# A new order of the words that drive all engines in a fused cross-attention kernel, with other places for its loads

## The chip, the cores and the metric

The kernel runs on one core of a Trainium2 chip. The metric is the device time of one execution in microseconds (us), as the median of several runs. Engines are named as in the profile: PE is TensorE (PEld its weight loads), DVE is VectorE, ACT ScalarE, POOL GpSimd, and SP is SyncE, which here issues nearly all DMAs.

## The reference

Everything is fp32: x is 2 x 2048 x 640, the context 2 x 154 x 1024, of which 77 rows are text and 77 image prompt. There are 20 heads of 32. Two softmaxes over 77 keys each are summed:

```python
q = _split_heads(hidden_states @ Wq.T, H)
k = _split_heads(text @ Wk.T, H)
v = _split_heads(text @ Wv.T, H)
out_text = _merge_heads(_attend(q, k, v, sm_scale))
k_ip = _split_heads(ip @ Wk_ip.T, H)
v_ip = _split_heads(ip @ Wv_ip.T, H)
out_ip = _merge_heads(_attend(q, k_ip, v_ip, sm_scale))
out = out_text + IP_SCALE * out_ip
out = out @ Wo.T + bo
return out + residual
```

## The kernel before

**Tiling.** Channels stand on the partitions. The work is cut into 10 pairs q (batch x chunk of 128 channels, that is four heads), each pair into two units u = 2q, 2q + 1 (half of the 2048 tokens), and each unit's eight 128-token tiles into three groups s (three, three and two tiles). Scores of a group lie in four PSUM banks, one per head (`halves`, or single `banks`); the softmax rows lie in SBUF in `pb`, 128 x 1848 for a group of three. The values of a pair are spread into the buffer `v4_0` or `v4_1` (by the pair's parity), as blocks for the attention run. The output product (Wo) uses sums of blocks of both factors, so that fewer products are needed; this part ends the program.

**The order.** Nothing here is scheduled by the framework. After a head that is written out (L523 to L558: the first loads, 40 small matmuls and projections), the string `SCHEDULE` (L561 to L625) holds one word for each step, and `emit` (L631) issues the instructions of a word in the order of the string. Each engine takes its own instructions in that order, so the string sets the order on PE, DVE, ACT, POOL and SP's DMA queue at once; semaphores add the waits for data and for buffers that come free. The words that are spoken of below:

- `Rs.u@h`: scores of group s of unit u (`scores`, L225), 24 matmuls, or 16 for group 2 (L232)
- `q.u.h`: query projection for 512 tokens, 5 chunks, which are 10 matmuls in the trace (`queries`, L197; L200), and `cq` its copy on ACT
- `k.c.t`, `v.c.t`: key and value projection of a chunk (`project_kv`, L137; L141), with `ck`, `cv` the copies
- `A.q`: the attention run of a pair (`attend`, L324; L331), 160 matmuls of 32 x 32 weights; `CA.q` its copy
- `K` copy of scores from PSUM to SBUF (L244, ACT), `M` maximum (L280, DVE), `S` subtraction of it (L294, POOL), `E` exponential (L300, or one by one with a bias, L268, ACT), `D` sum (L305, DVE), `I` reciprocal (L310), `N` normalisation (L315, POOL), `T` transposition (L322, DVE)
- `m`, `o`, `p`, `z`, `F`: products and sums of the output stage; `G`, `W` sums of blocks for it; `SF`, `SS` fetch and store of parts of the output, 256 KB each
- loads on SP: `LQ.q` a chunk of Wq into one of three buffers `wq_0` to `wq_2` (L191, 320 KB), `LK.n` a projection weight into one of four parts of `aT` (L131, 512 KB), `LX.u.h` a block of x of the second batch into one of `x_0` to `x_2` (L185, 1280 KB), `LO` all of Wo (L163, 1600 KB), `VS.q.half` eight small DMAs that spread v into the buffer `v4` of the pair (L157, 20 KB each; they wait until the run of pair q - 2 has read it)

A load waits on SP for its buffer, and everything behind it on SP waits with it. `DIRECT`, `BIASED` and `SUMMED` choose for a group how its softmax is taken: DIRECT reads scores from PSUM without the copy, BIASED leaves out the subtraction and gives the maximum as a bias to the exponential, SUMMED lets the exponential add up the rows.

Of the kernel before, what the change touches and what calls it, by code (L numbers as in the profile page):

```python
# [9 lines left out]
F32 = mybir.dt.float32  # L10
# [10 lines left out]
def kernel(  # L21
# [43 lines left out]
        (11, 0), (12, 0), (13, 0), (13, 2), (14, 0), (14, 2), (15, 1), (15, 2), (16, 2), (18, 1), (19, 2),  # L65
    }
    BIASED = {
        (3, 2), (4, 2), (5, 2), (6, 0), (8, 2), (9, 2), (10, 2), (12, 2), (18, 2),
    }
    SUMMED = {  # L70
        (4, 2), (10, 2), (12, 0), (12, 2), (13, 0), (13, 2), (14, 0), (15, 1), (15, 2), (16, 2), (18, 1),
        (18, 2),
# [480 lines left out]
    for t in range(2):  # L553
# [216 lines left out]
    for c, stages in enumerate(chains_of):  # L770
        for _, text in stages:
            for _, t in terms(text):
                for h in range(NH):
                    o = int(t[0]), NH * int(t[1]) + h
# [115 lines left out]
```

## Time and profile before

| what | value |
|---|---|
| median of 3 runs | 500.02 us (499.75 to 500.19) |
| profiled execution | 503.24 us |
| its span | 501.4 us |
| granted TensorE clock, mean | 0.997 |
| PE busy | 492.5 us |
| instructions in the trace | 10438 |

The span is the time from the first to the last record of the trace, and 1.8 us of the profiled execution lie around it. Rows of instruction groups read: line, engine, operation, output <- input, count, busy time and mean of one, then the idle time before it and what ended it. The chain rows read: start, length, engine, output, line, count. The rows on SP show DMA issues: start, length, engine, line, output <- input, count. q8 is the queue that brings TensorE its instructions, in packets.

### The profile page before, as it was taken

The numbers are of one execution on the slowest core, as the hardware profiler recorded it, in microseconds if no ns is written. First come the engines' busy times: TensorE is split into PE (matmuls) and PEld (weight loads), VectorE is DVE, ScalarE is ACT, GpSimd is POOL, SyncE is SP. The second block draws the span as 40 slices with busy tenths as digits, with TensorE's granted clock in tenths as the row PEclk, the third lists the DMA queues.
The fourth block names the chain that finished last, engine by engine and source line by source line (L and its number), as shares of the span: only waits on it lengthen the run. The fifth ranks groups of instructions, "written<-read, shape, count | busy, mean of one in ns | idle before, by whom it ended". The sixth has DMA issues, their size and how long they took to land.

```text
span 501.4 us, 10438 instructions
## 1 busy us (share of the span) xinstructions
PE 492.5 (98%) x4114; PEld 289.9 (58%) x4114; DVE 410.4 (82%) x411; ACT 303.2 (60%) x967; POOL 377.0 (75%) x167
## 2 busy tenths in 40 slices
PE   8999999999999989999999999999999999999996
PEld 4666658567457547446646654666655685444442
DVE  0069989979999987978997887678799999989785
ACT  1166768977797776757989887586677961100000
POOL 0069999878979886969976678556899899686950
PEclk9999999999999998999999999999999999999999
DMA  8991351060253560476552666653661122310125
GB/s 253 354 291 37 107 158 43 22 186 2 54 154 121 169 216 5 144 259 230 179 190 77 187 195 250 176 177 94 218 184 42 44 86 86 127 63 22 42 84 209
DMA packets 67473, 69.38 MB, mean 138 GB/s; under 512 B 5472, under 2 KB 47200, under 8 KB 67424
## 3 DMA queue, kind: packets, MB, share of 16 engines
q1 hardware_dynamic: 66704, 68.00, 43.1%
q8 instruction: 32, 0.52, 0.5%
q10 hardware_dynamic: 720, 0.72, 0.4%
q14 instruction: 17, 0.14, 0.1%
HBM read 54.94 MB, written 10.49 MB: 130 GB/s over the span
## 4 chain that ended last, share of the span: by engine, by line
PE 94%; DMA 3%; SPq 1%; issue 1%; ACT 0%; DVE 0%
PE bank L200 32%; PE bank L847 11%; PE bank L331 11%; PE bank L232 11%; PE bank L489 10%; PE bank L141 9%; PE bank L470 7%; PE bank L499 3%; DMA aT<-in_L_xattn_Wk_ip_dram 2%; DMA wq<-in_L_xattn_Wq_dram 2%; SPq L533 1%; SPq L131 0%; DVE x L793 0%; ACT pb L244 0%; ACT kT L558 0%
## 5 line engine op out<-in xcount | busy, mean ns | idle before, releaser
L315 POOL TENSOR_TENSOR pb<-pb,rden 128x1848 f32<-128x1848 f32 (+1 forms) x60 | 176.2, 2942 | 34.2 <-DVE rden L310 32.7
L200 PE MATMUL bank<-x,wq 128*128 128x512 f32 x400 | 179.5, 598 | 1.2 <-DMA wq<-in_L_xattn_Wq_dram 0.6
L294 POOL TENSOR_TENSOR pb<-pb,mx 128x1848 f32<-128x1848 f32 (+1 forms) x40 | 124.0, 3108 | 57.3 <-DVE mx L280 57.0
L200 PEld LDWEIGHTS bank<-x,wq 128*128 128x128 f32 x400 | 73.8, 190 | 87.1 <-issue 78.0
L322 DVE STREAM_TRANSPOSE pb<-pb 128x1920 f32<-128x1920 f32 (+1 forms) x60 | 116.1, 1940 | 6.0 <-POOL pb L315 5.5
L280 DVE TENSOR_REDUCE mx<-pb 128x24 f32<-128x1848 f32 (+1 forms) x49 | 90.4, 1854 | 34.8 <-ACT pb L244 34.6
L244 ACT COPY pb<-bank 128x462 f32<-128x462 f32 (+1 forms) x196 | 83.9, 543 | 32.4 <-PE bank L232 31.9
L305 DVE TENSOR_REDUCE den<-pb 128x24 f32<-128x1848 f32 (+1 forms) x48 | 90.1, 1883 | 14.0 <-ACT pb L300 13.8
L300 ACT ACTIVATE pb<-pb 128x1848 f32<-128x1848 f32 (+1 forms) x40 | 67.0, 1675 | 24.6 <-POOL pb L294 24.5
L268 ACT ACTIVATE pb<-bank,mx 128x77 f32<-128x77 f32 x224 | 64.0, 384 | 12.0 <-DVE mx L283 12.0
L232 PEld LDWEIGHTS bank<-kT,qT 32*128 32x128 f32 x1280 | 46.0, 185 | 29.7 <-issue 18.7
L232 PE MATMUL bank<-kT,qT 32*128 32x154 f32 x1280 | 57.5, 307 | 2.5 <-issue 2.2
L331 PE MATMUL bank<-pb,v 32*32 32x512 f32 x1600 | 55.5, 597 | 0.0
L141 PE MATMUL bank<-wo_ct,aT 128*128 128x154 f32 x320 | 47.1, 304 | 0.3 <-DMA aT<-in_L_xattn_Wk_ip_dram 0.3
L141 PEld LDWEIGHTS bank<-wo_ct,aT 128*128 128x128 f32 x320 | 44.4, 194 | 3.1 <-issue 2.1
L268 ACT ACTIVATE pb<-pb,mx 128x77 f32<-128x77 f32 x152 | 44.7, 389 | 1.1 <-DVE mx L280 1.1
L268 ACT ACTIVATION_READ_ACCUMULATOR pb<-bank,mx 128x1 f32 x168 | 43.6, 265 | 0.0
L331 PEld LDWEIGHTS bank<-pb,v 32*32 32x32 f32 x1600 | 30.0, 103 | 22.9 <-issue 12.9
L470 PE MATMUL bank<-aT,wo_ct 128*128 128x512 f32 x80 | 36.4, 596 | 0.0
L210 ACT ACTIVATE qT<-bank 128x512 f32<-128x512 f32 x40 | 23.9, 612 | 19.8 <-PE bank L200 19.7
L489 PE MATMUL bank<-aT,wo_ct 128*128 128x256 f32 x128 | 32.3, 387 | 0.0
L489 PEld LDWEIGHTS bank<-aT,wo_ct 128*128 128x128 f32 x128 | 23.6, 190 | 7.7 <-issue 4.0
(74 smaller groups left out, 439.1 us busy)
## 6 DMA issues: line engine op xcount, KB each, us to landing
x<-in_x_dram SPq DMA_DIRECT2D x20, 1280.0 KB, 7.5
out_dram<-acc SPq DMA_DIRECT2D x20, 256.0 KB, 3.0
x<-in_x_dram SPq DMA_DIRECT2D x18, 256.0 KB, 5.8
acc<-in_x_dram SPq DMA_DIRECT2D x16, 256.0 KB, 4.9
out_dram<-x SPq DMA_DIRECT2D x15, 256.0 KB, 2.1
v<-vS SPq DMA_DIRECT2D x160, 20.0 KB, 2.6
wq<-in_L_xattn_Wq_dram SPq DMA_DIRECT2D x9, 320.0 KB, 4.0
aT<-in_L_xattn_Wk_dram SPq DMA_DIRECT2D x5, 512.0 KB, 5.9
```

What stands on the lines that cost most here:

```text
L141: nc.tensor.matmul(keys_in(out), loaded[n][:, k, :], cT[:, k, :, t, :], start=(k == 0), stop=(k == NCC - 1))
L200: nc.tensor.matmul(pq, wqs[q % 3][:, k, :], xs[place_of(u, h)][:, k, :], start=(k == 0), stop=(k == NC - 1),)
L232: nc.tensor.matmul(ps[g][:, ts(t, 2 * L)], qTs[(u, h)][g * D : (g + 1) * D, ts(st, P)], kT[g * D : (g + 1) * D, c, b].rearrange("p t l -> ...
L244: nc.scalar.copy(keys_of(u, s)[:, :, g], ps[g][:, : n * 2 * L].rearrange("p (n l) -> p n l", n=n))
L268: nc.scalar.activation(row, row if ps is None else rows_in(ps[g], n)[:, t, x], AF.Exp, bias=maxs[(u, s)][:, *one], accum_out=None if den i ...
L280: nc.vector.tensor_reduce(mx, rows_of(u, s), AX.X, ALU.max, negate=negate)
L294: nc.gpsimd.tensor_tensor(rows_of(u, s), rows_of(u, s), maxs[(u, s)].unsqueeze(3).to_broadcast([P, n, 2, L]), ALU.subtract)
L305: nc.vector.tensor_reduce(den_of(u, s), rows_of(u, s), AX.X, ALU.add)
L315: nc.gpsimd.tensor_tensor(rows_of(u, s), rows_of(u, s), rdens[(u, s)].unsqueeze(3).to_broadcast([P, n, 2, L]), ALU.mult)
L322: nc.vector.transpose(p, p)
L331: nc.tensor.matmul(pa[r][g * D : (g + 1) * D, :], v4s[q % 2][rows, g, k, :], zones[rows, :, g, k, :], start=(k == 0), stop=(k == NK - 1),)
L489: nc.tensor.matmul(part, w_of[m][:, kp, op], t_of(m, b, i)[:, kp], start=(op == kp == 0 and m in (1, 2, 5)), stop=(op == 1 and kp == 1 and ...
```

## The change

`SCHEDULE` is replaced by another order of nearly the same words (1030 instead of 1025); everything that moves is in this string and in the three sets. TensorE has the same 4114 matmuls. There are 51 words K instead of 49, 42 S instead of 40, 49 D instead of 48. The head stays as it is. The new set `SUMMED` has one row less, so every line of the kernel after it has a number that is one less.

```diff
     DIRECT = {
-        (11, 0), (12, 0), (13, 0), (13, 2), (14, 0), (14, 2), (15, 1), (15, 2), (16, 2), (18, 1), (19, 2),
+        (11, 0), (12, 0), (13, 0), (13, 2), (15, 1), (15, 2), (16, 2), (18, 1), (19, 2),
     }
     BIASED = {
-        (3, 2), (4, 2), (5, 2), (6, 0), (8, 2), (9, 2), (10, 2), (12, 2), (18, 2),
+        (3, 2), (4, 2), (6, 2), (8, 2), (9, 2), (11, 2), (12, 1), (14, 0), (18, 2),
     }
     SUMMED = {
-        (4, 2), (10, 2), (12, 0), (12, 2), (13, 0), (13, 2), (14, 0), (15, 1), (15, 2), (16, 2), (18, 1),
-        (18, 2),
+        (4, 2), (11, 2), (12, 0), (13, 0), (13, 2), (14, 0), (15, 1), (15, 2), (18, 1), (18, 2), (19, 2),
     }
```

One line of the string, at the third attention run, from before and of the change:

```diff
-        "N1.7 M0.8 R1.8@1 q.10.0@2 K1.8 LX.11.0 T1.7 S0.8 M1.8 E0.8 A.3@1 LX.10.1 D2.8 S1.8 cq.9.1 D0.8 cq.10.0 "
+        "M0.8 R1.8@1 G5.0 q.10.0@3 LX.11.0 T1.7 K1.8 S0.8 cq.9.1 M1.8 E0.8 A.3@1 D2.8 S1.8 cq.10.0 D0.8 I0.8 E1.8 "
```

**SP around the run A.1.** Before, in the order of SP's DMAs: the spreads of pair 1, then `LQ.4`, `LK.14`, `LK.12`, `LQ.5`, `LK.11`, and spreads of pair 2. `LQ.5` and `LK.11` stand behind the word A.1 in the string, the three before them ahead of it.

```order
L157 DMA v4_1_81<-vS0_1_94 32x160 x16
L191 DMA wq_1_76<-in_L0_xattn_Wq_dram 128x5x128
L131 DMA aT_86<-in_L0_xattn_Wv_dram 128x8x128
L131 DMA aT_86<-in_L0_xattn_Wk_dram 128x8x128
L191 DMA wq_2_77<-in_L0_xattn_Wq_dram 128x5x128
L131 DMA aT_86<-in_L0_xattn_Wv_ip_dram 128x8x128
L157 DMA v4_0_80<-vS0_0_93 32x160 x8
```

After, at the same place (the first row is the second half of pair 1's spreads): `LK.14`, `LK.12` and `LQ.5` stand ahead of A.1, and the next load, `LK.15`, behind the run and the scores that follow it.

```order
L156 DMA v4_1_81<-vS0_1_94 32x160 x8
L130 DMA aT_86<-in_L0_xattn_Wv_dram 128x8x128
L130 DMA aT_86<-in_L0_xattn_Wk_dram 128x8x128
L190 DMA wq_2_77<-in_L0_xattn_Wq_dram 128x5x128
L130 DMA aT_86<-in_L0_xattn_Wv_ip_dram 128x8x128
L156 DMA v4_0_80<-vS0_0_93 32x160 x8
```

`LQ.4` has moved behind A.1, some rows further down, and `LQ.5` ahead of the run. On TensorE the projection right ahead of A.1 is `q.6.0` (buffer `wq_0`) where it was `q.5.1` (buffer `wq_2`); `q.5.1` now stands ahead of the scores `R1.4`.

**SP from the run A.3 to the run A.4.** Before: half of pair 3's spreads, then `LX.11.0` and `LX.10.1` (x_2, x_0), the first ahead of A.3, the second right behind it; the spreads of pair 4 around `LX.12.0`; then, ahead of A.4, a fetch, `LX.12.1` and `LO`, and the spreads of pair 5.

```order
L157 DMA v4_1_81<-vS0_1_94 32x160 x8
L185 DMA x_2_84<-in_x_dram 128x5x512
L185 DMA x_0_82<-in_x_dram 128x5x512
L157 DMA v4_0_80<-vS0_0_93 32x160 x8
L185 DMA x_1_83<-in_x_dram 128x5x512
L157 DMA v4_0_80<-vS0_0_93 32x160 x8
L458 DMA res_88<-in_x_dram 128x512
L185 DMA x_2_84<-in_x_dram 128x5x512
L163 DMA wo_ct_96<-in_L0_xattn_Wo_dram 128x5x640
L157 DMA v4_1_81<-vS1_95 32x160 x16
```

After: the spreads of pair 3, `LX.11.0`, half of pair 5's spreads, `LX.10.1`, `LQ.6`, `LX.12.0`, the sixteen spreads of pair 4, and then, ahead of A.4, `LX.12.1`, `LO`, `LX.13.0` and `LX.14.0`; the last row, `LX.13.1`, stands behind the run.

```order
L156 DMA v4_1_81<-vS0_1_94 32x160 x16
L184 DMA x_2_84<-in_x_dram 128x5x512
L156 DMA v4_1_81<-vS1_95 32x160 x8
L184 DMA x_0_82<-in_x_dram 128x5x512
L190 DMA wq_0_75<-in_L0_xattn_Wq_dram 128x5x128
L184 DMA x_1_83<-in_x_dram 128x5x512
L156 DMA v4_0_80<-vS0_0_93 32x160 x16
L184 DMA x_2_84<-in_x_dram 128x5x512
L162 DMA wo_ct_96<-in_L0_xattn_Wo_dram 128x5x640
L184 DMA x_0_82<-in_x_dram 128x5x512
L184 DMA x_1_83<-in_x_dram 128x5x512
L184 DMA x_2_84<-in_x_dram 128x5x512
```

`LX.10.1` has moved past the spreads of pair 5, which wait for the run A.3, since that run reads the buffer `v4_1`. `LX.13.0` and `LX.14.0`, which stood behind the word A.4 and the spreads of pair 5, now stand ahead of that run. Around A.7, `LX.18.1` stands behind the run's word in both orders, and in the new one right behind the eight spreads of `VS.8.0`, which stood some words further up.

124 rows, old and new, of the table SCHEDULE are left out of this document.

## The prediction

> **What bounds the kernel now.** I read the page's busy times first, then the shares of the chain that ended last, then what TensorE (PE) waited for.
>
> ```profile
> PE 492.5 (98%) x4114; PEld 289.9 (58%) x4114; DVE 410.4 (82%) x411; ACT 303.2 (60%) x967; POOL 377.0 (75%) x167
> ...
> PE 94%; DMA 3%; SPq 1%; issue 1%; ACT 0%; DVE 0%
> ...
> PE bank L232 <- issue: 2.2, 2, 1.7
> ```
>
> TensorE is busy for 98% of the span and the chain is TensorE for 94%. The 4114 matmuls are the same before and after, so only three things can move the time: pauses of TensorE, its clock, and what it pays at the joints between kinds of work. The third row is the largest pause behind the head: two waits in the scores, 2.2 us together, for nothing that the profile shows ("issue"). The timeline of TensorE gives their places, the windows what lies between them (columns: length; busy us and instructions of PE, PEld, DVE, ACT, POOL; granted clock; DMA share; GB/s):
>
> ```profile
> 113.80 0.53 PE L232 MATMUL bank<-kT,qT 32*128 32x154 f32 x3 [0.52 <-issue]
> ...
> 187.93 0.54 PE L232 MATMUL bank<-kT,qT 32*128 32x154 f32 x8 [1.65 <-issue]
> ...
> 113.80:187.93 74.13, 72.48 (x764) 44.82 (x764) 69.59 (x54) 58.47 (x142) 63.40 (x23) 1.00 0.39 121
> ...
> q8 instruction: 32, 0.52, 0.5%
> ```
>
> Between the two pauses TensorE has 764 recorded matmuls and as many weight loads, 1528 instructions. The queue of the last row carried 32 packets, 0.52 MB, so 16 KB each. TensorE's 4114 matmuls and 4114 weight loads over 32 give 257 a packet, and 1528 is six times 255. So I take both pauses to be at the edge of an instruction packet that came late. Both are in the scores behind an attention run (A.1, A.3), where 320 instructions pass in 5.45 us, so a packet lasts some 4.4 us instead of ten or more. Why late? SyncE's issues, the traffic by windows and the two runs in the chain answer:
>
> ```profile
> 102.01 0.58 SPq L191 DMA_DIRECT2D wq<-in_L_xattn_Wq_dram  x1
> ...
> 106.87 0.37 SPq L191 DMA_DIRECT2D wq<-in_L_xattn_Wq_dram  x1
> 107.28 0.53 SPq L131 DMA_DIRECT2D aT<-in_L_xattn_Wv_ip_dram  x1
> ...
> 180.12 0.37 SPq L185 DMA_DIRECT2D x<-in_x_dram  x1
> ```
> ```profile
> 102.00:104.00 2.00, 2.00 (x9) 1.14 (x8) 2.00 (x2) 2.00 (x7) 0.99 (x1) 1.00 0.22 55
> 104.00:106.00 2.00, 2.00 (x6) 0.94 (x5) 2.00 (x2) 0.10 (x1) 2.00 (x1) 1.00 1.10 319
> ...
> 108.00:110.00 2.00, 2.00 (x73) 1.29 (x63) 1.90 (x1) 1.51 (x5) 1.68 (x1) 1.00 0.97 272
> 110.00:112.00 2.00, 2.00 (x74) 1.11 (x58) 0.99 (x3) 1.53 (x2) 1.34 (x1) 1.00 0.73 197
> 112.00:114.00 2.00, 1.48 (x35) 1.03 (x24) 1.89 (x3) 2.00 (x8) 1.95 (x1) 1.00 0.04 10
> ...
> 184.00:186.00 2.00, 2.00 (x66) 1.00 (x44) 0.61 (x1) 2.00 (x4) 1.99 (x1) 1.00 0.80 305
> 186.00:188.00 2.00, 0.35 (x15) 0.23 (x9) 2.00 (x2) 1.54 (x6) 2.00 (x2) 1.00 0.04 8
> ```
> ```profile
> 106.84 5.45 PE bank L331 x154
> ...
> 180.09 5.45 PE bank L331 x149
> ```
>
> At A.1 a load of wq and one of a projection weight go out at the run's own start, behind loads that began to go out at 102.01 and are still landing. The DMA share (the last column but one) stays full until 0.73 of the window from 110, about 111.4. TensorE resumes 2.4 us later. At A.3 a block of x goes out at 180.12, the share ends at about 185.6 (0.80 of the window from 184), and TensorE resumes 2.3 us later. Two pauses with one distance from the end of the traffic: the packet waits behind the loads in the DMA engines, and its fetch takes some 2.35 us until TensorE runs.
>
> **The change part by part.** The working is against the profiled execution (503.24 us; span 501.4, 1.8 around it). What the pauses cost, in rows of the chain and one window:
>
> ```profile
> 112.29 0.98 PE bank L232 x21
> ...
> 114.33 4.41 PE bank L141 x32
> ...
> 185.54 0.73 PE bank L232 x16
> ...
> 188.47 6.07 PE bank L141 x32
> ...
> 209.14 1.04 PE bank L232 x24
> ...
> 352.67 5.72 PE bank L331 x154
> ```
> ```profile
> 188.62:192.03 3.41, 3.41 (x15) 3.41 (x15) 3.41 (x4) 1.65 (x4) 1.54 (x2) 0.50 0.02 5
> ```
>
> *A.1's loads.* The scores behind A.1 run from 112.29 to 114.33, 2.04 us; 24 such matmuls take 1.04 without a pause (209.14), 1.00 in other places. Cost: **1.04**. After the change the projection right ahead of A.1 is another (q.6.0 for q.5.1), so a wq buffer is free one projection earlier, and 512 + 512 + 320 KB go out some 4.4 us ahead of the run, none in it. Before, the loads issued from 102.01 flow from about 103.6 (0.22 of the window from 102). After, then, they flow from 2.8 us ahead of the run; 1344 KB at the 272 KB/us of the window from 108 take 4.9 us and end 2.1 into it. With the 2.4 of above TensorE could go on 4.5 us into the run; the pause of before began at 113.27, 6.4 into it. Margin 1.9 us: **-1.04**.
>
> *A.3's block.* Its scores run from 185.54 to 188.47, 2.93, so 1.93 too long. The two projections behind take 6.07 instead of the 4.41 of their like at 114.33, for the granted clock was 0.50 for 3.41 us. Cost: 1.93 + 1.66 = **3.59**. After, the block that went out at the run's start (LX.10.1) stands behind the spreads of VS.5.0, which wait for the run. There stays the block ahead of the projection (LX.11.0), 1280 KB, about 4 us ahead of the run. Two such blocks ended 5.5 us into it; without the second's 1280 KB at the 305 KB/us of the window from 184, 4.2 us less, they end 1.3 into it, and the pause came 6.2 into it. Margin over 2 us: **-3.59**.
>
> *A.7.* Its run takes 5.72, not 5.45, with a load of x at its start; after, eight spreads (VS.8.0) stand right ahead of that load on SyncE, so that it goes out later: **-0.27**.
>
> *Joints.* A projection takes 4.29 or 4.49:
>
> ```profile
> 164.07 4.29 PE bank L200 x10
> ...
> 170.11 4.49 PE bank L200 x10
> ```
>
> The longer one lies between scores or runs on both sides, 0.1 for each joint. The projections have 46 such joints before and 45 after: **-0.1**.
>
> Sum: 1.04 + 3.59 + 0.27 + 0.1 = **5.0**, and 503.2 - 5.0 = 498.2 for a profiled execution. The profiled one stands 3.2 above the median of the three timed runs (500.02), which is nearly the price of A.3; whether those have that pause cannot be seen. I take the sum off the median: 500.0 - 5.0 = 495.0.
>
> *What is added.* Five words that are no TensorE work: two more copies of scores (K), two more subtractions (S), one more sum (D), mostly as two steps (step 14) now go the way over SBUF. And all that TensorE gains must be kept by the engines beside it:
>
> ```profile
> L294 POOL TENSOR_TENSOR pb<-pb,mx 128x1848 f32<-128x1848 f32 (+1 forms) x40 | 124.0, 3108 | 57.3 <-DVE mx L280 57.0
> ...
> L305 DVE TENSOR_REDUCE den<-pb 128x24 f32<-128x1848 f32 (+1 forms) x48 | 90.1, 1883 | 14.0 <-ACT pb L300 13.8
> ...
> 69.60:180.00 110.40, 109.88 (x1161) 68.92 (x1160) 102.58 (x78) 89.69 (x229) 93.58 (x32) 1.00 0.34 98
> ...
> 210.17 0.53 ACT pb L244
> ```
>
> The two subtractions are 6.2 us of GpSimd and the sum 1.9 us of VectorE, in a stretch where these have idle time (377 and 410 of 501 us busy in all), so I cost them at nothing; if one is late by its whole length it costs up to 3.1. From A.0 to A.3 VectorE is busy for 102.58 of 110.40 us, 93%. One wait of TensorE for a ScalarE copy, 0.53 (at 210.17), is on the chain of before; it may go (-0.5). The bounds of the new waits are -0.5 and +3.1; I take two such as the 0.53, the nearest row, **+1.0**. That gives 495.0 + 1.0 = **496.0**.
>
> **A place where the change adds loads.** Just ahead of A.4 the new order sends out four loads instead of two:
>
> ```profile
> 211.51 0.38 SPq L185 DMA_DIRECT2D x<-in_x_dram  x1
> 211.93 0.52 SPq L163 DMA_DIRECT2D wo_ct<-in_L_xattn_Wo_dram  x1
> ```
> ```profile
> 216.31 5.45 PE bank L331 x149
> ```
> ```profile
> 218.00:220.00 2.00, 2.00 (x85) 1.40 (x67) 1.76 (x1) 0.21 (x1) 2.00 (x1) 1.00 1.03 408
> 220.00:222.00 2.00, 2.00 (x61) 0.90 (x31) 1.67 (x2) 0.92 (x1) 2.00 (x2) 1.00 0.85 298
> ...
> 187.93:227.50 39.57, 39.48 (x380) 23.10 (x380) 30.77 (x24) 25.92 (x55) 29.96 (x11) 0.96 0.40 131
> ...
> x<-in_x_dram SPq DMA_DIRECT2D x20, 1280.0 KB, 7.5
> ```
>
> Three packets (768 instructions; 760 are recorded) behind the pause at 187.93, the next edge of this kind is at 227.5, 11.2 us into A.4. Before, 2880 KB (a block of x and Wo) end at 221.7, 5.4 into the run; with 2.4 more TensorE has its packet 7.8 into it, 3.4 early. After, LX.13.0 and LX.14.0 add 2560 KB: at 408 KB/us 6.3 us. A packet behind all of it comes 14.1 into the run, 2.9 late; one that passes part of the queue, in time. The pauses of before had at most 2560 KB under way, part of it landed when the packet's turn came; the trace can't say that a packet waits for twice as much. I take nothing here for the forecast, and the full price for the rival.
>
> **A rule that speaks against all of it.** The Trainium skill, "DMA: Bandwidth & Descriptors", section "Queues, rings and completion order", has each DMA engine take turns between its queues, switching after at most 64 descriptors; the instruction queue would then wait for its turn and not for the loads to end. By that rule A.4 costs nothing, and, if the turn is short, the pauses at A.1 and A.3 were not the loads' doing and stay. The trace agrees with it little: both ended 2.3 to 2.4 us after the traffic did. "Runtime: NRT & Kernel Launch" of the Trainium skill, section "Instruction fetch mechanics", has TensorE hold 2048 instructions and calls the cost of an edge mostly hidden; the two pauses, six packets apart, were not.
>
> **The rivals.** *A.4's packet waits for everything (22%).* 2.9 us late by the rows; sixteen spreads of v stand together ahead of these loads instead of eight, so they may go out later against the run, and I add 1 us, an estimate. An idle of 1.65 was followed by 1.66 lost at half clock (A.3), one of 0.52 by nothing; so 3.9 + 1.7 = 5.6, and 496.0 + 5.6 = **501.6**, slower. It decides from the point where over 3.4 us of traffic more lie ahead of the packet than before. For it: both restarts followed the end of the traffic; against: the depth is new.
>
> *The timed runs lack A.3's pause (13%).* Then only 1.04 + 0.27 + 0.1 = 1.4 go: 498.6, or 499.6 with the new waits. For it: the 3.2 between profile and median.
>
> *VectorE and GpSimd become the bound (13%).* TensorE, now up to 5 us earlier, waits for scores' rows one subtraction longer (3.1): 495.0 + 3.1 = 498.1, and twice that 501.2. For it: the 93%; against: one wait of 0.53 behind the head before.
>
> *The change doesn't do what it says (8%).* Something else than the loads holds up TensorE's packets at the same two places: 500.0, give or take 1. For it: the packets have a queue of their own; against: the two equal distances from the end of the traffic. The two pages named above stand behind this case.
>
> **How the numbers follow.** The forecast, 496.0, has 44%: its own range is 493.6 (no new wait, the 0.53 gone, and the joints by up to 0.8 better) to 498.2. Over 0.2% (1.0 us), about what a measurement can tell from no change, faster is under 499.02 and slower over 501.02. Faster: nearly all of the forecast's 44, 8 of the 13 without A.3's pause, 6 of the 13 by VectorE, 2 from A.4 at part of its price: 60%. Slower: 15 of the 22 at A.4, 4 by VectorE, 2 from the last, 1 from the forecast: 22%. Between: 18%. The range is 493.6 to 502.0: below it the sum has nothing, and above lie A.4 with new waits as well.
>
> **What would show it.** In the profile after, the row of waits for "issue" in the scores is gone, and A.3's two projections take 4.41 at a clock of 1.00: the sum's two large terms. In A.1 and A.3 the DMA share falls under 0.2 within 2.5 us of the run's start. A pause in the first product or score behind A.4, 11 us into it, is the rival's sign; new waits for "ACT pb" or "POOL pb" ahead of scores and runs are VectorE's. Wrong altogether is the argument if pauses stay where no load is under way, or go where the loads are as before.

## The result and the profile after

The changed kernel takes 497.19 us (median of 6, 496.59 to 498.4), the kernel before 499.9 (6 runs, 499.75 to 500.69): a ratio of 0.9945, 95% interval 0.9931 to 0.996. The forecast was 496.0, faster; the measured gain is 2.7 us where 4.0 were forecast. The profiled execution went from 503.24 to 497.84 us, 5.4 less, where the sum for it was 5.0 ahead of the charge for new waits. The difference between these two gains is the main question below. In one experiment, A.1's loads alone, two of twelve executions, the profiled one among them, took 631 and 2840 us and are left out.

From the page and TensorE's waits of the changed kernel:

```profile
span 496.0 us, 10378 instructions
...
PE 489.1 (99%) x4114; PEld 288.5 (58%) x4114; DVE 413.0 (83%) x417; ACT 301.4 (61%) x929; POOL 370.3 (75%) x158
...
PE bank L199 <- DMA x<-in_x_dram: 1.4, 1, 1.4
PE bank L547 <- DVE pb L545: 1.1, 1, 1.1
```

No "issue" wait in the scores is left; the largest waits that remain stand in the head. The chain of the changed kernel at A.1, A.3 and A.7 (start, length, work):

```profile
106.83 5.45 PE bank L330 x151
112.28 1.00 PE bank L231 x24
...
179.02 5.45 PE bank L330 x152
184.47 1.00 PE bank L231 x24
185.47 4.41 PE bank L140 x32
...
346.13 5.45 PE bank L330 x153
```

The scores behind A.1 and A.3 take 1.00 instead of 2.04 and 2.93, the two projections 4.41 instead of 6.07, and A.7 takes 5.45 instead of 5.72 (more on A.7 below). The windows around both runs (the last columns are the granted clock, the DMA share and GB/s), then SyncE's issues:

```profile
108.00:110.00 2.00, 2.00 (x73) 1.26 (x64) 0.87 (x2) 0.54 (x2) 2.00 (x2) 1.00 0.50 118
110.00:112.00 2.00, 2.00 (x74) 1.09 (x58) 0.62 (x1) 1.42 (x2) 2.00 (x1) 1.00 0.00 0
...
180.00:182.00 2.00, 2.00 (x82) 1.38 (x68) 2.00 (x2) 0.72 (x2) 2.00 (x1) 1.00 0.78 298
182.00:184.00 2.00, 2.00 (x79) 1.23 (x60) 0.87 (x3) 1.46 (x1) 1.56 (x2) 1.00 0.00 0
```
```profile
102.57 0.38 SPq L130 DMA_DIRECT2D aT<-in_L_xattn_Wv_dram  x1
102.99 0.58 SPq L130 DMA_DIRECT2D aT<-in_L_xattn_Wk_dram  x1
103.62 1.29 SPq L190 DMA_DIRECT2D wq<-in_L_xattn_Wq_dram  x1
...
176.02 0.53 SPq L184 DMA_DIRECT2D x<-in_x_dram  x1
...
189.29 0.58 SPq L184 DMA_DIRECT2D x<-in_x_dram  x1
```

The three loads of A.1 go out ahead of the run and the traffic ends at 109.0, 2.2 us into it (before: 111.4). At A.3 one block goes out at 176.02, LX.10.1 only at 189.29, and the traffic ends at 181.6 (before: 185.6).

At A.4 the four loads went out together (the third of the last row's blocks is LX.13.1, behind the run), and TensorE did not pause:

```profile
208.93 0.53 SPq L184 DMA_DIRECT2D x<-in_x_dram  x1
209.50 0.52 SPq L162 DMA_DIRECT2D wo_ct<-in_L_xattn_Wo_dram  x1
210.12 11.86 SPq L184 DMA_DIRECT2D x<-in_x_dram  x3
```
```profile
221.00:223.00 2.00, 2.00 (x27) 1.13 (x26) 1.94 (x2) 1.68 (x1) 2.00 (x1) 1.00 1.06 391
223.00:225.00 2.00, 2.00 (x6) 0.95 (x5) 2.00 (x5) 1.73 (x9) 1.92 (x3) 1.00 1.05 386
```
```profile
211.64 5.45 PE bank L330 x149
...
221.58 1.00 PE bank L231 x24
222.58 4.49 PE bank L469 x10
```

The DMA share stays full to 225, more than 13 us after the run's start at 211.64. Three packets behind the edge at A.3, the next edge lies at about 224.8 in this trace, 13.1 us into the run and not 11.2, in the product of L469, which takes its plain 4.49. The trace also has the time at which the packet on q8 was moved: from 216.46 to 217.55, while the DMA share was 1.03 (window from 216 to 218). So it came through in spite of traffic that had not ended.

### The profile page after: what moved, and what is told of

Same layout as the page of the kernel before. It is cut to its first block, busy times and chain, and to the rows that moved or that the text cites. A ratio compares the mean times of both kernels' runs of the same rounds, so it can differ in the third digit from the quotient of the medians.

```text
span 496.0 us, 10378 instructions
## 1 busy us (share of the span) xinstructions
PE 489.1 (99%) x4114; PEld 288.5 (58%) x4114; DVE 413.0 (83%) x417; ACT 301.4 (61%) x929; POOL 370.3 (75%) x158
## 4 chain that ended last, share of the span: by engine, by line
PE 95%; DMA 3%; SPq 1%; ACTq 0%; ACT 0%; DVE 0%; issue 0%
PE bank L199 33%; PE bank L846 11%; PE bank L330 11%; PE bank L231 11%; PE bank L488 10%; PE bank L140 9%; PE bank L469 7%; PE bank L498 3%; DMA aT<-in_L_xattn_Wk_ip_dram 2%; DMA x<-in_x_dram 1%; SPq L532 1%; ACTq L526 0%; SPq L130 0%; DVE acc L792 0%; ACT pb L243 0%
## 5 line engine op out<-in xcount | busy, mean ns | idle before, releaser
L293 POOL TENSOR_TENSOR pb<-pb,mx 128x1848 f32<-128x1848 f32 (+1 forms) x42 | 128.2, 3066 | 58.5 <-DVE mx L279 58.3
L279 DVE TENSOR_REDUCE mx<-pb 128x24 f32<-128x1848 f32 (+1 forms) x51 | 93.8, 1850 | 32.0 <-ACT pb L243 31.8
L243 ACT COPY pb<-bank 128x462 f32<-128x462 f32 (+1 forms) x204 | 87.1, 537 | 34.6 <-PE bank L231 34.0
L304 DVE TENSOR_REDUCE den<-pb 128x24 f32<-128x1848 f32 (+1 forms) x49 | 91.5, 1875 | 18.6 <-ACT pb L299 15.8
L299 ACT ACTIVATE pb<-pb 128x1848 f32<-128x1848 f32 (+1 forms) x42 | 69.3, 1651 | 18.6 <-POOL pb L293 18.5
L267 ACT ACTIVATE pb<-bank,mx 128x77 f32<-128x77 f32 x184 | 53.1, 380 | 10.8 <-DVE mx L282 10.8
L267 ACT ACTIVATE pb<-pb,mx 128x77 f32<-128x77 f32 x160 | 47.3, 373 | 0.0
L140 PE MATMUL bank<-wo_ct,aT 128*128 128x154 f32 x320 | 45.8, 297 | 0.4 <-DMA aT<-in_L_xattn_Wk_ip_dram 0.4
L140 PEld LDWEIGHTS bank<-wo_ct,aT 128*128 128x128 f32 x320 | 42.8, 188 | 3.4 <-issue 2.2
L267 ACT ACTIVATION_READ_ACCUMULATOR pb<-bank,mx 128x1 f32 x144 | 36.7, 258 | 0.0
L469 PE MATMUL bank<-aT,wo_ct 128*128 128x512 f32 x80 | 36.4, 595 | 0.0
```

The lines of the kernel that those rows point to most:

```text
L140: nc.tensor.matmul(keys_in(out), loaded[n][:, k, :], cT[:, k, :, t, :], start=(k == 0), stop=(k == NCC - 1))
L243: nc.scalar.copy(keys_of(u, s)[:, :, g], ps[g][:, : n * 2 * L].rearrange("p (n l) -> p n l", n=n))
L267: nc.scalar.activation(row, row if ps is None else rows_in(ps[g], n)[:, t, x], AF.Exp, bias=maxs[(u, s)][:, *one], accum_out=None if den i ...
L279: nc.vector.tensor_reduce(mx, rows_of(u, s), AX.X, ALU.max, negate=negate)
L293: nc.gpsimd.tensor_tensor(rows_of(u, s), rows_of(u, s), maxs[(u, s)].unsqueeze(3).to_broadcast([P, n, 2, L]), ALU.subtract)
L304: nc.vector.tensor_reduce(den_of(u, s), rows_of(u, s), AX.X, ALU.add)
```

## The experiments

Two theories were to be told apart. **End of traffic**: a packet waits until the loads queued ahead of it have all landed; this is what the prediction said of A.1 and A.3. **Bounded**: it waits for a part of the queue that does not grow with the queue's depth. Beside them stood the question what each run's loads bring in ordinary executions. Ratios are to the kernel before on the same chip, with the 95% interval.

**The kernel before again** (no edit).

> The kernel before, unchanged, to see its other executions beside the profiled one of 503.24 us. If the pause behind A.3 and the half clock after it belong to every execution, the mean clock is 0.997 in all of them and the chain again shows 1.65 us of issue. If most executions lack them, the median stays near 499.9 with a mean clock of 1.00, and the 3.3 us between 503.24 and 499.9 are A.3's price.

Measured: 0.9997 (0.998 to 1.0015). Its twelve executions take 499.46 to 503.71 us. The two with a mean clock of 0.997 or less take 502.43 and 503.71, the fastest has a clock of 1.00; but 501.69 and 502.01 come with 1.00 and 0.999, so the clock is not all that varies. The execution whose profile was taken (499.93 us, clock 1.00) has both pauses in its chain:

```profile
111.51 0.98 PE bank L232 x21
112.50 0.51 issue
113.01 0.53 PE bank L232 x3
...
184.75 0.74 PE bank L232 x16
185.48 1.06 issue
186.54 0.54 PE bank L232 x8
```

A.1's scores again take 2.02; A.3's take 2.34 with a pause of 1.06, not 1.65, and the clock does not fall. So neither of the two outcomes that were expected: the pause is there in an ordinary execution, its half clock is not. The two cost 1.02 + 1.34 = 2.4 us here, against 1.04 + 3.59 in the profiled execution on which the sum was made.

**A.3's load alone.**

```diff
-A.3@1 LX.10.1 D2.8 ... R0.9@0 CA.3 D1.8 ... K2.10 LO VS.5.0 T1.9
+A.3@1 D2.8 ... R0.9@0 VS.5.0 CA.3 LX.10.1 D1.8 ... K2.10 LO T1.9
```

> The kernel before with one part of the change: LX.10.1 goes out behind A.3 and behind the spreads of VS.5.0. If A.3's pause is in the timed executions: 1.9 to 3.6 us faster (about 496.3 to 498.0). If only the profiled one had it: within 0.3 us of before. In the profile no issue wait behind A.3 by either; a pause at the same place would mean that the load was not its cause.

Measured: 498.32 us, 0.9949 (0.9927 to 0.9971), 2.6 us. The scores behind A.3 take 1.00. One load, moved behind eight small ones, brings most of the gain of the whole new order. In this execution A.1's scores take 1.45, a smaller pause than in the other profiles, so 2.6 (1.5 to 3.7 by the interval) is not A.3's share alone.

**A.1's loads alone.**

```diff
-N1.3 VS.1.1 ... M0.4 LQ.4 q.5.1@1 ... A.1@1 LQ.5 LK.11 cq.5.1 ... N0.5 VS.2.1 D2.5
+N1.3 LK.11 LQ.4 VS.1.1 ... M0.4 q.5.1@1 ... A.1@1 cq.5.1 ... N0.5 VS.2.1 LQ.5 D2.5
```

> The kernel before with LK.11 and LQ.4 sent out earlier and LQ.5 behind the spreads of pair 2, so that no load goes out at the start of A.1. By the sum of the prediction 1.0 us faster (about 498.9), with no issue wait behind A.1. The rival, that this pause is hidden in timed executions: within 0.3 us of before.

Measured: 500.42 us (median of ten executions), 0.9985 (0.9968 to 1.0001): the interval excludes neither no gain nor the 1.0 us that were expected. There is no profile of these ten. The next kernel shows where the gain can go.

**Both** (the two edits together).

> Both moves of loads and nothing else of the new order. If the late packets are all that the change mends: as fast as the changed kernel, 497.2, give or take 0.5. If the rest of the new order brings something too, slower than the changed one by that much, up to 499; if the rest costs something, 495.3 to 496.5.

Measured: 498.71 us, 0.9949 (0.9933 to 0.9964), no better than A.3's part alone. The chain at A.2 and the windows there:

```profile
143.24 5.45 PE bank L331 x154
148.68 0.72 PE bank L232 x12
149.41 0.53 issue
149.94 0.79 PE bank L232 x12
```
```profile
148.00:150.00 2.00, 1.47 (x42) 0.63 (x16) 2.00 (x2) 1.68 (x4) 2.00 (x1) 1.00 0.93 326
150.00:152.00 2.00, 2.00 (x22) 1.84 (x23) 2.00 (x3) 1.85 (x5) 1.75 (x2) 1.00 0.73 274
```

A new pause of the same kind stands behind A.2, whose three loads (LQ.6, LK.17, LX.10.0) the kernel before sends out in the run. In this profile what A.1 gives is given back one run later: A.1's scores take 1.00, A.2's 2.04. And the pause ends at 149.94 while the DMA goes on until about 151.5: the first sign against the end of traffic.

**All three runs.** A.2's loads are moved too:

```diff
-M2.6 LK.16 T2.5 ... A.2@1 LQ.6 LK.17 I2.6 LX.10.0 E1.6 ... k.4.1@6 LK.19 M0.7
+M2.6 LK.17 LK.16 T2.5 ... A.2@1 I2.6 E1.6 ... k.4.1@6 LK.19 LX.10.0 LQ.6 M0.7
```

> The order of before with the loads of A.1, of A.2 and of A.3 moved out of the runs. The last experiment showed that without A.1's pause a pause of 0.5 us comes behind A.2, whose loads now stand in the packet's way. If late packets are all that the change mends: no issue wait anywhere and the time of the changed kernel, give or take 0.4 us. If the rest of its order brings something: above that by as much.

**The changed kernel again**, in the same comparison (no edit).

> The changed kernel, unchanged, beside the kernel before on the same chip: the ratio of the result again, 0.993 to 0.996, with no issue wait in the scores. Its executions should lie closer together than those of before (0.3% against up to 0.9%), if the late packets are what makes those vary.

Measured: 497.58 us for the order of before with its loads moved out of three runs, 0.993 (0.9904 to 0.9955); 497.1 for the changed kernel, 0.9928 (0.9901 to 0.9955). They are 0.5 us apart, where 0.4 was allowed for, but within the intervals these are one time. Seven loads and one group of spreads moved in the old order do what the whole new order does; the sets, the other places of the softmax's words and the five extra words bring and cost nothing that can be measured. The executions of both lie closer together (497.19 to 498.46 and 496.59 to 498.51) than those of before (498.94 to 504.68). Neither profile has an issue wait behind the three runs; the kernel with the three edits:

```profile
111.07 1.00 PE bank L232 x24
...
148.18 1.00 PE bank L232 x24
...
183.29 1.00 PE bank L232 x24
```

**A.1 and A.2 without A.3**, to see whether the parts add up.

> The kernel before with the loads of A.1 and A.2 moved out of the runs and A.3's load left in. If the pauses add up: 0.9 to 1.1 us faster than before (A.1's price), no issue wait behind A.1 and A.2, and the pause of 0.8 to 1.65 us still behind A.3. If A.3's pause grows when TensorE comes earlier: no faster than before.

Measured: 499.22 us, 0.9972 (0.9959 to 0.9984), 1.4 us (0.8 to 2.1), and this is the measured price of A.1. The pause behind A.3 is there, 0.98 us ("185.40 0.98 issue" in its chain). 1.4 and the 2.6 of A.3's part make 4.0, where all three together gave 3.5 (0.993 of 500.5): additive within the intervals.

**The one load put back** into the changed kernel.

```diff
-A.3@1 D2.8 ... N1.8 LX.10.1 R2.9@0
+A.3@1 LX.10.1 D2.8 ... N1.8 R2.9@0
```

> The changed kernel with LX.10.1 put back right behind the word A.3, ahead of the spreads of VS.5.0, and nothing else. If this load makes the packet behind A.3 late: the issue wait is back in the scores behind A.3 and the time is 1.3 us (a pause alone) to 3.6 us (with the half clock) above the changed kernel. If it takes the loads of the other runs as well to do harm: no more than 0.3 us.

Measured: 498.71 us against 497.1 for the changed kernel in the same comparison, +1.6; 0.9951 (0.9931 to 0.9972) of before. The pause is back in its chain, without a half clock:

```profile
178.54 5.45 PE bank L330 x154
183.99 0.85 PE bank L231 x17
184.84 0.96 issue
185.80 0.54 PE bank L231 x7
```

**Less of it.** 512 KB of that load behind A.3, the other 768 KB behind VS.5.0 (`LH` loads the first two chunks of the block, `LX.10.1` the other three).

```diff
-A.3@1 D2.8
+A.3@1 LH.10.1 D2.8
```

> The changed kernel with 512 of the 1280 KB of LX.10.1 put back right behind A.3, the other 768 KB staying behind VS.5.0. The whole load there cost 1.36 us in the scores, with a wait of 0.96. If the packet waits for what is queued ahead when its turn comes: 768 KB less at some 400 KB/us are 1.9 us less, so no issue wait and the time of the changed kernel within 0.3 us. If any load at the start of the run delays the packet by a fixed amount: the wait of about 1 us and 1.4 us in time are back.

Measured: 497.58 us, 0.9941 (0.9926 to 0.9956), a ratio like the changed kernel's (0.9945 and 0.9928). The scores behind A.3 take 1.00:

```profile
178.06 5.45 PE bank L330 x154
183.51 1.00 PE bank L231 x24
```

This does not show that the amount alone counts, for the time of the load moved too. The 512 KB went out at 175.55, 2.5 us ahead of the run (they overwrite only two chunks of the buffer, which are presumably free earlier), while the whole block of the last experiment went out at 178.57, at the run's start. The packet on q8 was moved from 181.40, 3.3 us into the run: later than the 2.3 of the changed kernel, earlier than the 4.7 with the whole block, and in time.

**More of it.** The kernel before with one more load of 1280 KB, which nobody reads, between LX.11.0 and LX.10.1.

```diff
-K1.8 LX.11.0 T1.7
+K1.8 LX.11.0 LD T1.7
+        elif k == "LD":
+            nc.sync.dma_start(out=xs[XROOM], in_=xT[:, ds(S, TB)].rearrange("(k p) t -> p k t", p=P))
```

> The kernel before with one more load of 1280 KB (a block of x that nobody reads, into the buffer that is free since q.9.1) between LX.11.0 and LX.10.1, so that it is queued ahead of A.3's packet. If a packet waits until the traffic ahead of it ends: the pause behind A.3 grows by 1280 KB at some 390 KB/us, 3.3 us, to 4 to 5 us, and the time by 3.3 to 5 us. If a packet waits for a bounded part of the queue: the pause stays within 0.6 us of the 1.1 to 1.65 seen without it, and ends while the DMA share is still full.

Measured: 500.33 us, 0.999 (0.9967 to 1.0013): the load costs nothing that can be measured (up to 0.7 us by the interval). Its issues, its chain and its windows at A.3:

```profile
176.99 0.53 SPq L185 DMA_DIRECT2D x<-in_x_dram  x1
177.62 0.47 SPq L651 DMA_DIRECT2D x<-in_x_dram  x1
179.87 0.37 SPq L185 DMA_DIRECT2D x<-in_x_dram  x1
```
```profile
185.29 0.74 PE bank L232 x16
186.03 1.22 issue
187.25 0.54 PE bank L232 x8
```
```profile
184.00:186.00 2.00, 2.00 (x60) 1.00 (x41) 0.86 (x1) 2.00 (x5) 2.00 (x1) 1.00 1.05 388
186.00:188.00 2.00, 0.78 (x14) 0.59 (x10) 2.00 (x2) 1.59 (x6) 2.00 (x2) 1.00 1.05 386
188.00:190.00 2.00, 2.00 (x17) 2.00 (x17) 2.00 (x2) 1.59 (x4) 1.26 (x1) 1.00 0.61 219
```

The pause is 1.22 us, between the 1.06 and the 1.65 without the load, and TensorE goes on at 187.25 in a window with a full DMA share; the traffic ends 2 us later, at 189.2. The end of traffic as the rule falls; the bounded wait holds.

**The packets in the traces.** The profiles also hold the times at which q8's packets are moved, and these show directly what the counts of instructions only suggested. Six profiles have pauses behind A.1, A.2 or A.3, nine in all: before, before again, both, A.1 and A.2, the load put back, and more of it. Each pause ends 1.3 to 1.6 us after a packet of q8 has been moved, which takes 1.0 to 1.2 us. With TensorE's semaphore instructions counted beside its matmuls and weight loads, all nine end at instruction 1984, 2752 or 3520 of the trace, give or take one: these are three times 256 apart, so they are edges of packets. Where no pause follows, the packet starts to move 1.5 to 3.8 us into the run (at 3.8, behind A.1 in the kernel with A.3's load alone moved, the scores took 1.45); where one follows, 4.2 to 5.3 us. With the extra load, A.3's packet is moved from 184.73 to 185.82, among loads that fill the DMA engines and go on to 189.2:

```profile
q1 hardware_dynamic: 210, 0.41, 99.8%
q8 instruction: 1, 0.02, 6.2%
```

So the packet is late, and it is not the end of the loads that it waits for.

## Why the prediction was right, and where it was not

*Late packets behind A.1 and A.3, made late by loads* (the reading of the profile): shown. The pause goes when A.3's load is moved and comes back when it alone is put back, and each pause ends just behind a packet of q8, at an edge of 256 instructions. What failed in this step is the wait itself: "behind the loads", for some 2.35 us from their end until TensorE runs. In the traces TensorE runs 1.3 to 1.6 us after the packet has been moved, and the packet can be moved while the loads still flow.

*A.1: -1.04.* The size was right (2.02 in the scores of the second profile, 1.00 after; 1.4, between 0.8 and 2.1, by the experiment), though other executions show 1.45 in the scores, or a pause of 0.87. The traffic ended 2.2 us into the run where 2.1 was worked out. What the step did not see is that this gain needs A.2's loads moved as well. The change does that too, but the prediction didn't count it: with A.1 and A.3 mended, A.2 paused by 0.53.

*A.3: -3.59.* The place was right, the size not. The step took a profiled execution with a pause of 1.65 and 3.41 us at half clock; an ordinary one has a pause of 1.06 and no half clock, 1.34 in all, and putting the load back costs 1.6. The traffic ended 2.5 us into the run, not 1.3, and that was early enough. This term is 2.0 to 2.3 us too large. It is the rival "the timed runs lack A.3's pause" in a milder form: they lack its half clock and a part of the pause. The 3.2 us between profile and median pointed there, and the sum was nevertheless taken off the median.

*A.7: -0.27.* The run takes 5.45 after the change, but also in the second profile of the kernel before, where the load stands as it did, and 5.95 in that with A.3's load alone. So this term is not the load's; why the run takes longer in some executions stays open. The joints' 0.1 is too small to be seen.

*New waits: +1.0.* There were none to count: from A.0 to A.3 VectorE is now busy for 102.44 of 109.42 us,

```profile
69.60:179.02 109.42, 109.42 (x1169) 68.61 (x1174) 102.44 (x78) 85.50 (x207) 98.02 (x34) 1.00 0.35 99
```

and TensorE for all of them. The row that gave the size was misread. The 0.53 at 210.17 is time of a ScalarE copy on the chain, and TensorE did sixteen scores of another group meanwhile: it was idle for 0.09 us of the window from 210 to 211. The changed kernel has the same row, 0.53 at 205.51. In another execution of the changed kernel TensorE waited once for VectorE, 0.7 us ahead of a product at 386; so this rival has a place, but it does not decide.

*The sum.* With the second profile's terms it is 1.02 + 1.34 = 2.36 and a few tenths for the joints and small waits, and 2.7 was measured. The forecast of 4.0 came from a term 2.2 too large and a charge of 1.0 that did not fall due: two errors that partly cancelled. That the number came out as near as it did is in part luck. The 2.7 is itself one sample (2.0 to 3.4 by its interval): compared again, with executions of before that hold longer pauses, the gain was 3.6 (2.3 to 5.0).

*A.4.* The price of 5.6 in the rival rested on the packet waiting for everything. It doesn't; the queue was as deep as was worked out, and later (full beyond 13 us into the run, where its end was worked out at 11.7), and the packet passed. To take nothing for it in the forecast was right, but the mechanism that the prediction wrote down for A.1 and A.3 ("behind the loads") would have charged it. The two equal distances of 2.3 and 2.4 us from the traffic's end were what misled: in those two cases little traffic was left when the packet had its turn (it began to move at 111.18 and 185.36, and the traffic ended at 111.4 and 185.6). The Trainium skill, "DMA: Bandwidth & Descriptors", section "Queues, rings and completion order", with its engines that take turns between queues after a bounded number of descriptors, fits these runs: the wait did not grow with 1280 KB more. The prediction drew from it that, if the turn is short, the pauses are not the loads' doing. The turn is not short: beside full queues the packets of the nine pauses began to move 4.2 to 5.3 us into a run, instead of about 2, and that is too late when a packet is used up in 4.4 us.

## What to carry to other kernels

Where TensorE runs short instructions back to back, look for "issue" pauses at equal counts of instructions and for the instruction packets in the trace, and put large loads so that little is queued when such a run begins: here 1280 KB issued 3 us ahead, and 512 KB more 2.5 us ahead, did no harm, and 1280 more at its start cost 1.4 to 1.6 us. Mend all such runs at once, since a gain in one can move the collision to the next. And price a pause from more than one execution: the profiled one may hold the rare form.

## What the runs showed of the hardware

The instruction queue does not wait for the data queue to drain: a packet came through while the DMA share was 1.05, and a deeper queue did not lengthen the pause (1.22 against 1.06 to 1.65). In one execution TensorE's clock fell to half for 3.41 us after an idle time of 1.65 us; in the others it did not after 0.53, 0.96, 1.06 or 1.22. What sets the length of the bounded wait, descriptors, bytes or time, stays open: the runs only show that the rest of a block with 512 KB sent out 2.5 us ahead of the run leaves the packet in time, and with 1280 KB sent out at its start does not.
